# A recommendation kernel on one core: at most three gathers in flight, in place of eight

## The chip, the cores and the metric

The kernel runs on one NeuronCore of one Trainium2 chip. The core has a tensor engine (PE) for matrix products and transposes, a vector engine (DVE), a scalar engine (ACT) for activations, GpSimd (POOL), and a synchronisation engine (SP). SP, ACT and POOL can issue DMA transfers. In this kernel every gather of table rows is issued by POOL[...]; the 16 DMA engines of the core then move the rows. A semaphore tells when a transfer has landed.

The metric is device time in microseconds (us) of one launch, from the first to the last instruction. "The time before" is the median of three timed executions. Beside these stands one execution taken by the hardware profiler, with its own time.

## The reference

The model scores 16384 users (`B`), each with a target item and a history of 100 items (`L`), out of 50001 items (`ITEMS`). Every item has 32 neighbours. First each item gets two 32-wide vectors by attention over its neighbours, once for each of two tables; then each user is scored with a small attention network over the history.

```python
def _neighbor_attn(E, near_full):
    V = E[near_full]                                   # 50001 x 32 x 32
    scores = jnp.einsum('nd,nkd->nk', E, V) / jnp.sqrt(jnp.float32(GEO_HALF))
    w = jax.nn.softmax(scores, axis=-1)
    return jnp.einsum('nk,nkd->nd', w, V)
...
h = jnp.concatenate([E_hist[history], hist_bi], axis=-1)   # B x 100 x 128
t = jnp.concatenate([E_tgt[target], tgt_bi], axis=-1)      # B x 128
x = h * t[:, None, :]
z = jax.nn.relu(jnp.einsum('bld,hd->blh', x, W1) + b1)
scores = jnp.einsum('blh,h->bl', z, W2[0])
exp_A = jnp.exp(scores)
mask = (history != target[:, None]) & (history != 0)
exp_A = exp_A * mask
denom = jnp.sum(exp_A, axis=-1) ** BETA
...
s = jnp.sum(result)                # one number over all users
pred = dot / (n1 * n2)             # cosine of t with a vector of s
return jax.nn.sigmoid(pred)
```

All arithmetic is float32.

## The kernel before

The kernel has two stages and a short tail. Everything is laid out over 128 partitions.

**Stage 1, items.** 23 iterations (`NITER`) each cover 128 x 17 items (`NSUB` = 17). An iteration loads the neighbour indices (`nidx`), the items' own rows (`own`) and the history embeddings (`row`) by SP. For each of its 17 subtiles, 32 gathers (L111) bring one neighbour each for 128 items into a tile `v` of a five-buffer pool (64 floats a row). DVE multiplies (L120), reduces, ACT takes the exponentials, and DVE forms the weighted sum (L145, L152). At the end of an iteration SP writes the finished rows to two tables in DRAM, `table` (L163) and `ttab` (L164). There are 391 subtiles and so 12512 gathers. At the very start ACT also issues a 12.5 MB copy of the target embeddings into `ttab` (L91).

**Stage 2, users.** 128 users at a time, 128 such columns (`UC`). For each column one gather (L197) brings the target's rows `t`, and 100 gathers (L233) bring the history's rows, four to a group (`LG` = 4), 25 groups to a column (`NG`), into tiles `h` of a twelve-buffer pool (128 floats a row). That is 12800 gathers `h` and 128 gathers `t`, 25440 gathers in all with stage 1. A group then goes through:

- `turn`: four transposes on PE into `hT_ps` (L246), a DVE product with the transposed target into `xT` (L248), and a DVE row sum `hsum` (L249);
- `hidden`: a 128x128 by 128x512 product on PE into `z_ps` (L255), and a ReLU on ACT into `z` (L257);
- `scored`: four products on PE, one column each, into `score` (L265).

In the source these three stand one group apart (groups s, s-1 and s-2 in one turn of the loop). The program's layer that schedules the kernel takes this recording, decides in which order each engine gets its instructions by its own account of when their inputs are ready, and then sets semaphore waits. Engines run their lists strictly in that order. In the built program before, PE's usual order of a turn is: two transposes of a group, the first transpose of the next group, the first score product, a further transpose, three score products, and the product for `z`.

**Gathers in flight.** The layer gives the gathers eight semaphores in rotation. A gather waits until the gather eight places before it, the last user of its semaphore, has landed; the first eight of stage 1 wait for no gather. Where a tile's buffer is used again, the first gather into it also waits for the engines that read the old contents. Gathers run on POOL in the order of the program, and nothing else of weight runs on POOL.

Of the kernel before, what the change touches and what calls it, by code (L numbers as in the profile page):

```python
# [15 lines left out]

P = 128
ITEMS = 50001
K = 32
G = 32  # L20
DE = 64
# [8 lines left out]
NSUB = 17  # L30
NITER = -(-ITEMS // (P * NSUB))
ROWS = NITER * P * NSUB
# [10 lines left out]
def kernel(  # L43
# [11 lines left out]
    out: bass.AP,  # L55
):
    nc = tc.nc

    const = ctx.enter_context(tc.tile_pool(name="const", bufs=1))
    dram = ctx.enter_context(tc.tile_pool(name="dram", bufs=1, space=bass.MemoryType.DRAM))  # L60
# [29 lines left out]

    nc.scalar.dma_start(ttab[0 : ITEMS - 1, 0:DE], etgt[0 : ITEMS - 1, :])  # L91
    nc.scalar.dma_start(ttab[ITEMS - 1 : ITEMS, 0:DE], etgt[ITEMS - 1 : ITEMS, :])
    with (
        tc.tile_pool(name="n_in", bufs=2) as n_in,
        tc.tile_pool(name="n_v", bufs=5) as n_v,
        tc.tile_pool(name="n_p", bufs=2) as n_p,
        tc.tile_pool(name="n_s", bufs=3) as n_s,
        tc.tile_pool(name="n_ps", bufs=2, space=bass.MemoryType.PSUM) as n_ps,
    ):
        for it in range(NITER):  # L100
            nidx = n_in.tile([P, NSUB, K], I32, name="nidx")
            nc.sync.dma_start(nidx, near_v[it])
            own = n_in.tile([P, NSUB, 2 * G], F32, name="own")
            nc.sync.dma_start(own, egeo_v[it])
            row = n_in.tile([P, NSUB, D], F32, name="row")
            nc.sync.dma_start(row[:, :, 0:DE], ehist_v[it])
            trow = n_in.tile([P, NSUB, 2 * G], F32, name="trow")
            for j in range(NSUB):
                v = n_v.tile([P, K, 2, G], F32, name="v")
                for k in range(K):  # L110
                    nc.gpsimd.indirect_dma_start(  # L111
                        out=v[:, k].rearrange("p t d -> p (t d)"),
                        out_offset=None,
                        in_=egeo,
                        in_offset=bass.IndirectOffsetOnAxis(ap=nidx[:, j, k : k + 1], axis=0),
                    )
                own_ps = n_ps.tile([P, 1, 2 * G], F32, name="own_ps")
                nc.scalar.copy(own_ps[:, 0, :], own[:, j, :])  # L118
                prod = n_p.tile([P, K, 2, G], F32, name="prod")
                nc.vector.tensor_tensor(  # L120
                    prod.rearrange("p k t d -> p k (t d)"),
                    v.rearrange("p k t d -> p k (t d)"),
                    own_ps.to_broadcast([P, K, 2 * G]),
                    ALU.mult,
                )
                sc = n_s.tile([P, 2, K], F32, name="sc")
                nc.vector.tensor_reduce(sc.rearrange("p t k -> p k t"), prod, AX.X, ALU.add)  # L127
                top = n_s.tile([P, 2], F32, name="top")
                nc.vector.tensor_reduce(top, sc, AX.X, ALU.max)
                nc.vector.tensor_scalar(top, top, -scale, None, ALU.mult)  # L130
                ex = n_ps.tile([P, 2, K], F32, name="ex")
                tot = n_s.tile([P, 2, 1], F32, name="tot")
                for t in range(2):
                    nc.scalar.activation(  # L134
                        ex[:, t, :],
                        sc[:, t, :],
                        AF.Exp,
                        bias=top[:, t : t + 1],
                        scale=scale,
                        accum_out=tot[:, t, :],  # L140
                    )
                nc.vector.reciprocal(tot, tot)  # L142
                wv = n_p.tile([P, 2, G, K], F32, name="wv")
                for t in range(2):
                    nc.vector.tensor_tensor(  # L145
                        wv[:, t].rearrange("p d k -> p k d"),
                        v[:, :, t, :],
                        ex[:, t, :].rearrange("p (k o) -> p k o", o=1).to_broadcast([P, K, G]),
                        ALU.mult,
                    )  # L150
                att = n_s.tile([P, 2, G], F32, name="att")
                nc.vector.tensor_reduce(att, wv, AX.X, ALU.add)  # L152
                nc.vector.tensor_tensor(  # L153
                    row[:, j, DE:D].rearrange("p (t d) -> p t d", t=2),
                    att,
                    tot.to_broadcast([P, 2, G]),
                    ALU.mult,
                )
                for t in range(2):
                    nc.scalar.copy(  # L160
                        trow[:, j, t * G : (t + 1) * G], row[:, j, D - (t + 1) * G : D - t * G]
                    )
            nc.sync.dma_start(table_v[it], row)  # L163
            nc.sync.dma_start(ttab_v[it][:, :, DE:D], trow)  # L164
# [11 lines left out]
    with (  # L176
# [12 lines left out]
        def target_rows(c):  # L189

            if c % BSUB == 0:
                hidx = u_in.tile([P, BSUB, L], I32, name="hidx")
                nc.sync.dma_start(hidx, hist_v[c // BSUB])
                hists[c // BSUB] = hidx

            t = u_t.tile([P, D], F32, name="t")
            nc.gpsimd.indirect_dma_start(  # L197
                out=t,
                out_offset=None,
                in_=ttab[0:ITEMS, :],  # L200
                in_offset=bass.IndirectOffsetOnAxis(ap=tidx[:, c : c + 1], axis=0),
            )
            users[c] = {"t": t, "hidx": hists[c // BSUB][:, c % BSUB, :]}
# [24 lines left out]
        def gather(c, g):  # L228
            u = users[c]
            h = u_h.tile([P, LG, D], F32, name="h")  # L230
            for q in range(LG):
                l = g * LG + q
                nc.gpsimd.indirect_dma_start(  # L233
                    out=h[:, q, :],
                    out_offset=None,
                    in_=table,
                    in_offset=bass.IndirectOffsetOnAxis(ap=u["hidx"][:, l : l + 1], axis=0),
                )
            u["h", g] = h
# [37 lines left out]

        groups = [(c, g) for c in range(UC) for g in range(NG)]
        target_rows(0)
        for s in range(len(groups) + 2):  # L280
            if s < len(groups):
                c, g = groups[s]
                if g == 0:
                    target_work(c)
                if g == NG // 2 and c + 1 < UC:
                    target_rows(c + 1)
                gather(c, g)
                turn(c, g)
            if 1 <= s <= len(groups):
                hidden(*groups[s - 1])  # L290
            if s >= 2:
                scored(*groups[s - 2])
# [88 lines left out]
```

## Time and profile before

| | us |
|---|---|
| median of three timed runs | 36274.81 |
| lowest and highest of them | 36267.18, 36292.37 |
| the profiled execution's own time | 31810.23 |
| its span, first to last instruction | 31808.5 |
| stage 1 in the profile, first to last gather issue | 9.7 to 15626.3 |
| history gathers of stage 2, first to last issue | 15651.5 to 31787.6 |
| POOL busy in the span | 24005.7 (75%) |
| PE busy in the span | 15238.9 (48%, all but nothing of it in stage 1) |
| DVE busy | 8951.2 (28%) |
| ACT busy | 2851.2 (9%) |

The profiled execution took 4464.6 us less than the median of the timed runs. The page tells how the time of that one execution was spent; it tells nothing of how the timed ones differ from it.

A line of the groups reads: line of the kernel, engine, operation, what is written and read, how many | busy time in all, mean duration of one in ns | idle time of the engine just before them, and what ended most of it. In the digits of the 40 slices a 9 means 90% or more busy; the granted clock of PE is 1.0 in the first half and 0.5 for nearly all of the second. In the timeline a row begins with the start and the duration in us; several instructions of a kind are merged (x3), and brackets tell how long the engine had been idle and what ended it.

### The profile page before, as it was taken

The numbers are of one execution on the slowest core, as the hardware profiler recorded it, in microseconds if no ns is written. First come the engines' busy times: TensorE is split into PE (matmuls) and PEld (weight loads), VectorE is DVE, ScalarE is ACT, GpSimd is POOL, SyncE is SP. The second block draws the span as 40 slices with busy tenths as digits, with TensorE's granted clock in tenths as the row PEclk, the third lists the DMA queues.
The fourth block names the chain that finished last, engine by engine and source line by source line (L and its number), as shares of the span: only waits on it lengthen the run. The fifth ranks groups of instructions, "written<-read, shape, count | busy, mean of one in ns | idle before, by whom it ended". The sixth has DMA issues, their size and how long they took to land.

```text
span 31808.5 us, 154035 instructions
## 1 busy us (share of the span) xinstructions
PE 15238.9 (48%) x44931; PEld 9632.2 (30%) x44931; DVE 8951.2 (28%) x10957; ACT 2851.2 (9%) x6458; POOL 24005.7 (75%) x25446
## 2 busy tenths in 40 slices
PE   0000000000000000000299999999999999999999
PEld 0000000000000000000155555555555555555555
DVE  2222222222222222222222222222222222222222
ACT  0000000000000000000011111111111111111111
POOL 7777777777777777777777777777777777777777
PEclk9999999999999999999955555555555555555555
DMA  2111111111111111111122222222222222222221
GB/s 50 30 30 30 30 31 33 30 30 30 30 34 30 30 30 30 31 33 28 37 54 53 54 53 54 53 54 54 53 54 53 54 53 54 54 53 54 53 54 52
DMA packets 981064, 1358.75 MB, mean 43 GB/s; under 512 B 559872, under 2 KB 564352, under 8 KB 977280
## 3 DMA queue, kind: packets, MB, share of 16 engines
q0 software_dynamic: 814080, 1258.87, 17.1%
q1 hardware_dynamic: 115952, 77.16, 0.9%
q10 hardware_dynamic: 50192, 12.87, 0.2%
q8 instruction: 363, 5.95, 0.1%
q14 instruction: 477, 3.91, 0.0%
HBM read 1308.76 MB, written 51.30 MB: 43 GB/s over the span
## 4 chain that ended last, share of the span: by engine, by line
POOL 49%; issue 19%; PE 15%; DMA 14%; DVE 2%; ACT 1%; POOLq 0%; ACTq 0%; SPq 0%; DVEq 0%
POOL v L111 35%; POOL h L233 13%; DMA h<-table,hidx 11%; PE z_ps L255 7%; PE score L265 5%; PE hT_ps L246 3%; DMA v<-in_egeo_dram,nidx 2%; DVE xT L248 2%; ACT z L257 1%; POOL t L197 0%; POOLq L233 0%; DVE tT L211 0%; DVE ea L274 0%; DMA nidx<-in_near_dram 0%; DMA ttab<-trow 0%
## 5 line engine op out<-in xcount | busy, mean ns | idle before, releaser
L233 POOL DMA_INDIRECT h<-table,hidx x12800 | 12079.2, 944 | 3900.9 <-issue 3159.2
L111 POOL DMA_INDIRECT v<-in_egeo_dram,nidx x12512 | 11805.1, 943 | 3820.9 <-issue 3719.2
L209 PE MATMUL hT_ps<-ident,t 128*128 128x128 f32 x128 | 53.9, 421 | 15644.7 <-DMA t<-ttab,tidx 15644.7
L265 PEld LDWEIGHTS score<-w_sb,z 128*128 128x128 f32 x25600 | 6225.7, 334 | 1080.8 <-ACT z L257 1074.0
L255 PE MATMUL z_ps<-xT,w1T 128*128 128x512 f32 x6400 | 6526.7, 1123 | 0.0
L265 PE MATMUL score<-w_sb,z 128*128 128x1 f32 x25600 | 5903.9, 335 | 235.4 <-ACT z L257 150.2
L246 PE MATMUL hT_ps<-ident,h 128*128 128x128 f32 x12800 | 4715.0, 439 | 673.3 <-DMA h<-table,hidx 520.3
L249 DVE TENSOR_REDUCE hsum<-h 128x4 f32<-128x512 f32 x3200 | 2194.7, 686 | 9243.7 <-DMA h<-table,hidx 9226.9
L209 PEld LDWEIGHTS hT_ps<-ident,t 128*128 128x128 f32 x128 | 28.8, 225 | 15644.9 <-ACT idf L217 15644.9
L246 PEld LDWEIGHTS hT_ps<-ident,h 128*128 128x128 f32 x12800 | 2676.6, 209 | 5434.3 <-issue 3257.2
L120 DVE TENSOR_TENSOR prod<-v,own_ps 128x2048 f32<-128x2048 f32 x391 | 894.6, 2288 | 10794.7 <-DMA v<-in_egeo_dram,nidx 10794.4
L257 ACT ACTIVATE z<-z_ps,b_sb 128x512 f32<-128x512 f32 x3200 | 2199.1, 687 | 13448.3 <-PE z_ps L255 13335.1
L248 DVE TENSOR_TENSOR xT<-hT_ps,tT 128x512 f32<-128x512 f32 x3200 | 2210.2, 691 | 2028.6 <-PE hT_ps L246 2026.8
L255 PEld LDWEIGHTS z_ps<-xT,w1T 128*128 128x128 f32 x6400 | 1745.4, 332 | 0.0
L145 DVE TENSOR_TENSOR wv<-v,ex 128x1024 f32<-128x1024 f32 x782 | 1398.8, 1867 | 0.0
L118 ACT COPY own_ps<-own 128x64 f32<-128x64 f32 x391 | 84.4, 216 | 11499.9 <-DVE prod L120 11498.4
L127 DVE TENSOR_REDUCE sc<-prod 128x64 f32<-128x2048 f32 x391 | 894.5, 2288 | 13.4
L152 DVE TENSOR_REDUCE att<-wv 128x64 f32<-128x2048 f32 x391 | 893.8, 2286 | 13.4
L160 ACT COPY trow<-row 128x32 f32<-128x32 f32 x782 | 131.7, 215 | 2465.7 <-DVE row L153 2465.7
L134 ACT ACTIVATE ex<-sc,top 128x32 f32<-128x32 f32 x782 | 227.7, 291 | 1081.9 <-DVE top L130 1069.2
L142 DVE RECIPROCAL tot<-tot 128x2 f32<-128x2 f32 x391 | 64.8, 166 | 362.3 <-ACT ex L134 362.3
L197 POOL DMA_INDIRECT t<-ttab,tidx x128 | 120.7, 943 | 60.5 <-issue 60.5
(49 smaller groups left out, 808.6 us busy)
## 6 DMA issues: line engine op xcount, KB each, us to landing
h<-table,hidx POOLq DMA_INDIRECT x12800, 2.5
v<-in_egeo_dram,nidx POOLq DMA_INDIRECT x12512, 2.4
table<-row SPq DMA_DIRECT2D x23, 1088.0 KB, 4.4
own<-in_egeo_dram SPq DMA_DIRECT2D x23, 544.0 KB, 3.6
row<-in_ehist_dram SPq DMA_DIRECT2D x23, 544.0 KB, 6.7
ttab<-trow SPq DMA_DIRECT2D x23, 544.0 KB, 6.8
ttab<-in_etgt_dram ACTq DMA_DIRECT2D x1, 12500.0 KB, 53.5
hidx<-in_history_dram SPq DMA_DIRECT2D x32, 200.0 KB, 2.5
```

Source lines behind the costliest of these rows:

```text
L111: nc.gpsimd.indirect_dma_start(out=v[:, k].rearrange("p t d -> p (t d)"), out_offset=None, in_=egeo, in_offset=bass.IndirectOffsetOnAxis(a ...
L120: nc.vector.tensor_tensor(prod.rearrange("p k t d -> p k (t d)"), v.rearrange("p k t d -> p k (t d)"), own_ps.to_broadcast([P, K, 2 * G]), ...
L127: nc.vector.tensor_reduce(sc.rearrange("p t k -> p k t"), prod, AX.X, ALU.add)
L145: nc.vector.tensor_tensor(wv[:, t].rearrange("p d k -> p k d"), v[:, :, t, :], ex[:, t, :].rearrange("p (k o) -> p k o", o=1).to_broadcast ...
L152: nc.vector.tensor_reduce(att, wv, AX.X, ALU.add)
L233: nc.gpsimd.indirect_dma_start(out=h[:, q, :], out_offset=None, in_=table, in_offset=bass.IndirectOffsetOnAxis(ap=u["hidx"][:, l : l + 1], ...
L246: nc.tensor.transpose(hT_ps[:, q, :], h[:, q, :], ident)
L248: nc.vector.tensor_tensor(xT, hT_ps, u["tT"].to_broadcast([D, LG, P]), ALU.mult)
L249: nc.vector.tensor_reduce(u["hsum"][:, g * LG : (g + 1) * LG], h, AX.X, ALU.add)
L255: nc.tensor.matmul(z_ps, w1T, u["xT"].pop(g), start=True, stop=True)
L257: nc.scalar.activation(z, z_ps, AF.Relu, bias=b1_sb)
L265: nc.tensor.matmul(u["score"][:, l : l + 1], z[:, q, :], w2_sb, start=True, stop=True)
```

## The change

A wrapper, `gather_rows`, issues the gathers of all three places. It keeps a list of those issued, and from the fourth on it adds one dependency: the new gather waits until the gather three places before it has landed. The list runs over both stages. No instruction, no buffer and no transfer is added or taken away by the source; the layer that schedules the program sees the new dependencies when it decides the engines' orders, and drops waits that another one already covers.

```diff
+AHEAD = 3
...
+    issued = []
+    landed = mybir.DependencyInfo(mybir.DependencyClass.Sync, mybir.DependencyReason.DATA)
+
+    def gather_rows(**kw):
+        g = nc.gpsimd.indirect_dma_start(**kw)
+        if len(issued) >= AHEAD:
+            tc.add_manual_dep(g.ins, issued[-AHEAD].ins.name, landed, reason="AHEAD")
+        issued.append(g)
...
                 for k in range(K):
-                    nc.gpsimd.indirect_dma_start(
+                    gather_rows(
                         out=v[:, k].rearrange("p t d -> p (t d)"),
...
             t = u_t.tile([P, D], F32, name="t")
-            nc.gpsimd.indirect_dma_start(
+            gather_rows(
                 out=t,
...
                 l = g * LG + q
-                nc.gpsimd.indirect_dma_start(
+                gather_rows(
                     out=h[:, q, :],
```

In the built programs POOL has 25440 gathers before and after. Before, a gather's wait names the landing of the gather eight before it; after, that of the gather three before it, in the same place, so no wait is added in number (3745 waits that stand alone before, 3743 after). SP's order is unchanged. PE's order in stage 2 changes. After, most of it is a pattern that repeats every three groups (h a transpose, s a score product, digits the place in the group of four):

```
z(1)  h2.0 h2.1 h2.2  s1.0-s1.3  h2.3 h3.0 h3.1
z(2)  h3.2 h3.3       s2.0-s2.3  h4.0
z(3)  h4.1 h4.2 h4.3  s3.0-s3.3
z(4)  ...
```

Before, most turns are:

```
z(1)  h2.2 h2.3 h3.0  s1.0  h3.1  s1.1-s1.3
z(2)  h3.2 h3.3 h4.0  s2.0  h4.1  s2.1-s2.3
```

## The prediction

> **What bounds the kernel now.** I read the page's busy shares and chain first, then the groups, then one line's instructions, then the timeline.
>
> ```profile
> POOL 49%; issue 19%; PE 15%; DMA 14%; DVE 2%; ACT 1%; POOLq 0%; ACTq 0%; SPq 0%; DVEq 0%
> ...
> L233 POOL DMA_INDIRECT h<-table,hidx x12800 | 12079.2, 944 | 3900.9 <-issue 3159.2
> L111 POOL DMA_INDIRECT v<-in_egeo_dram,nidx x12512 | 11805.1, 943 | 3820.9 <-issue 3719.2
> ...
> h<-table,hidx POOLq DMA_INDIRECT x12800, 2.5
> v<-in_egeo_dram,nidx POOLq DMA_INDIRECT x12512, 2.4
> ```
>
> POOL leads the chain. A gather is busy 0.944 us and has an idle 0.30 us before it that ends by itself ("issue"), not by another's signal. The timeline shows the beat: starts at 6135-6145 below lie 1.25 us apart. Pace: (31787.6 - 9.7) us over 25440 gathers = 1.249 us, with a pause of only 23 us between the stages. The landing, 2.4 to 2.5 us from the start, comes after 2.45/1.249 = 2 beats. So about two gathers are in flight, although eight may be; it is POOL's issuing and not the limit that sets the pace.
>
> The exceptions are where large transfers share the DMA engines. For L111 between 6134 and 6146 us, and then from 9 to 52 us, its own rows say:
>
> ```profile
> DMA to landing us min/median/max: 2.5/4.3/5.5
> ...
> DMA to landing us min/median/max: 3.6/5.6/6.4
> ```
>
> ```profile
> 6134.74 0.33 SPq L163 DMA_DIRECT2D table<-row  x1
> 6134.93 0.94 POOL L111 DMA_INDIRECT v<-in_egeo_dram,nidx  x1 [0.30 <-issue]
> 6135.17 0.56 SPq L164 DMA_DIRECT2D ttab<-trow  x1
> 6136.18 0.94 POOL L111 DMA_INDIRECT v<-in_egeo_dram,nidx  x1 [0.30 <-issue]
> ...
> 6139.16 0.89 SPq L106 DMA_DIRECT2D row<-in_ehist_dram  x1
> ```
>
> Gathers land late beside the write-out of an iteration, and POOL keeps its beat nevertheless, since eight are allowed. In the first 52 us the 12.5 MB copy does the same.
>
> In stage 2 a second engine is close. The slices show PE at 9 with its clock at 5, and one turn of PE reads:
>
> ```profile
> 25001.99 2.06 PE L255 MATMUL z_ps<-xT,w1T 128*128 128x512 f32 x2
> 25003.83 0.85 PE L246 MATMUL hT_ps<-ident,h 128*128 128x128 f32 x3
> 25004.14 0.69 ACT L257 ACTIVATE z<-z_ps,b_sb 128x512 f32<-128x512 f32 x1 [4.63 <-PE z_ps L255]
> 25004.88 0.59 PE L265 MATMUL score<-w_sb,z 128*128 128x1 f32 x2 [0.20 <-ACT z L257]
> 25006.71 2.05 PE L255 MATMUL z_ps<-xT,w1T 128*128 128x512 f32 x2
> 25008.56 0.85 PE L246 MATMUL hT_ps<-ident,h 128*128 128x128 f32 x3
> 25008.87 0.69 ACT L257 ACTIVATE z<-z_ps,b_sb 128x512 f32<-128x512 f32 x1 [4.04 <-PE z_ps L255]
> 25009.23 0.69 DVE L248 TENSOR_TENSOR xT<-hT_ps,tT 128x512 f32<-128x512 f32 x1 [0.88 <-PE hT_ps L246]
> ```
>
> From three transposes to the next three is 4.73 us. The gathers allow a group 101 x 1.249/25 = 5.04 us (101 a column, 25 groups). PE has 0.31 us a group to spare.
>
> **What the Trainium skill says.** "DMA: Bandwidth & Descriptors", section "Anatomy of one DMA — SWDGE (gpsimd) path": about 2 us of a POOL-issued DMA is fixed, mostly completion, and engines of the DMA do not wait on semaphores; the issuer does. The trace agrees: 2.4 us of which 0.94 us is POOL's own. Same page, "Issuing engines are not separate DMA queues": SP's transfers interleave with POOL's on the same 16 engines; the 4.3 us beside the write-out agrees. "Perfetto Trace Analysis", section "DMA Instruction — SWDGE (GPSIMD)": the profiled end is that of descriptor writing, and an instruction sits in a wait queue until its semaphores are met, then in the execution queue. So the landing is to be taken from the issues' table, not from the 944 ns.
>
> **The change, part by part.**
>
> *The wait.* It replaces one; no instruction is added (25440 gathers, as many waits). Gather n may go when n-3 has landed. From the start of n-3: landing 2.45, plus about 0.28 us from signal to start (the first gather of all starts 0.28 us after the last semaphore event of its index transfer), together 2.73. Its turn comes after 3 x 1.249 = 3.75. It is met 1.0 us early, at no cost. What covers it is POOL's own work on the two gathers between; without it (two allowed, 2.50 of beats) each pair would lose 0.23 us. The wait queue of POOL holds only gathers behind this one.
>
> *Late landings.* Free up to 3.75 - 0.28 = 3.47 us. Beside each write-out some eight gathers land after about 4.5 us: three rounds of three, each 1.0 to 1.3 us late, 3 to 4 us an iteration; 23 iterations, 70 to 90 us. The first 44 us: a round takes 5.6 + 0.28 = 5.9 in place of 3.75, so 22 gathers go in place of 34: 15 us, some 20 with the loads just behind. At the profile's pace stage 1 loses about 100 us. POOL is the bound and nothing gives it back.
>
> *PE's order.* Signals from the rows above: `z` start to the scores that need it, 25004.88 - 25001.99 = 2.89 us. A transpose is 0.213 us of PE (three start at .213 spacing within the 0.85 row), four score products 1.71, `z` 1.85. From the start of a group's last transpose to its `xT` done and `z` starting: 0.46 + 0.69 + 0.06 = 1.21. Adding up the new three-group pattern: z, 3 transposes to 2.49, wait to 2.89 for ACT, scores to 4.61; last transpose then two others to 5.25, wait to 4.61 + 1.21 = 5.82 for DVE; z, two transposes to 8.10, wait to 5.82 + 2.89 = 8.71; scores to 10.43; one transpose; z at 10.64; three transposes, wait to 13.53; scores to 15.25. That is 5.08 us a group; before 4.73. So at the profile's pace PE passes POOL: (5.08 - 5.04) x 3200 = 130 us, and the target's transpose, once a column, is no longer hidden: up to 1 us x 128. Say 200 us, with late landings of stage 2 under it. Profile after: 31810 + 100 + 200 = 32,110.
>
> *At the pace of the timed runs.* They are 4465 us longer, 0.175 us a gather if spread over all. The page doesn't show where. If it is the beat of the gathers, it is 1.424 us: a group has 101 x 1.424/25 = 5.75 us, and PE's 5.08 is hidden by POOL again. Free landing grows to 4.27 - 0.28 = 3.99: beside a write-out rounds are 0.5 to 0.8 us late, 1.5 to 2.5 us an iteration, 35 to 58 us; at the start 22 gathers go in place of 31, 12 us; loads behind, 5 to 10. Sum 52 to 80, bounds 35 (signal to start at nothing) to 140 (nothing of it shrinks). I take 85, towards the slower side because the late gathers delay the tile that triggers the next write.
>
> **Rivals.**
> 1. *Forecast, 55%*: the beat is 1.42 us in timed runs. 36,275 + 85 = 36,360; its own range 36,310 to 36,415. For: two thirds of the chain is POOL and its issue; against: no view shows that beat.
> 2. *PE's new order shows, 22%*: stage 2 runs timed as profiled (the extra time lies in stage 1 or around). 100 + 200: 36,575, between 36,480 and 36,700.
> 3. *PE sets the timed runs' stage 2, 7%*: then 4.73 against 5.08 counts whole: 0.35 x 3200 = 1120, plus 100: 37,490. Against: PE would have to be over a third slower than at half clock.
> 4. *Landings are longer in timed runs, 8%*: from 3.99 us on, every 0.1 us costs 0.033 x 25440 = 850 us; at 4.1 us, 37,200.
> 5. *Faster, 6%*: the extra 0.175 us comes from gathers parked in POOL's queue, seven before and two after. It decides from 85/25440 = 0.0033 us a gather on; if a tenth goes, 0.0175 x 25440 = 445, less 85: 35,915. The profile's steady beat with the queue full speaks against it.
> 6. *Nothing happens, 2%*: landings beside the write-outs stay under the limit in timed runs: 36,275.
>
> **How the numbers follow.** 36,360 is case 1's. Cases 1, 2 and 6 hold 79%; a little of case 4 brings the range to 36,240 to 36,850. Within 0.2% (73 us, about what a measurement of this kernel can tell from no change): 42% of case 1, case 6 and a shred of 5, 0.26. Faster: 0.06. Slower: the rest, 0.68.
>
> **What would show it.** In the profile after, which has its own pace: L111's idle time is ended by "DMA v" for some 100 us at write-outs and in the first 52 us, and its plain beat stays 1.249; stage 2 longer by about 200 us, POOL waiting on buffers of `h`, PE waiting more for ACT `z` and for DVE `xT`. If POOL's beat is longer everywhere, the 0.28 us or the queue was misjudged. If stage 2 keeps 5.04 us a group, the PE sum is wrong. Timed runs beyond 36,480 make cases 2 to 4 likely; below 36,200, case 5.

## The result and the profile after

| | before | after |
|---|---|---|
| median of four timed runs each, us | 36275.44 | 36505.90 |
| lowest and highest, us | 36267.18, 36292.37 | 36500.71, 36511.53 |
| ratio, with its 95% interval | | 1.0063 (1.0046 to 1.0080) |

The change costs 230 us. The forecast was 36,360 in a range of 36,240 to 36,850. The time lies in the range, above the forecast's own range (36,310 to 36,415), and just inside the range of another case, that PE's new order shows (36,480 to 36,700).

The profile after was taken at the pace of these timed runs, whereas the profile before (31810.23 us) has the pace of the three chips of the experiments below, on which the unchanged kernel takes 31,808 us, timed as well as profiled; so the two profiles may not be subtracted from each other.

The page of the changed kernel, its busy times, its chain, the two groups of gathers and their issues:

```profile
PE 14440.2 (40%) x44931; PEld 9262.2 (25%) x44931; DVE 8694.6 (24%) x10957; ACT 2848.9 (8%) x6458; POOL 25501.7 (70%) x25446
...
PE 15%; another core or an unknown queue 12%; issue 4%; POOL 3%; DVE 2%; ACT 2%; DMA 1%; DVEq 0%; ACTq 0%; POOLq 0%
...
L65 POOL DMA_INDIRECT h<-table,hidx x12800 | 12078.1, 944 | 6655.3 <-issue 3380.1
L65 POOL DMA_INDIRECT v<-in_egeo_dram,nidx x12512 | 13302.2, 1063 | 4215.2 <-issue 4030.4
...
h<-table,hidx POOLq DMA_INDIRECT x12800
```

All gathers now have the wrapper's line, L65. The chain ends in releasers that the records do not name, and the landing that stood beside the issues before (2.5 us) is missing, because a part of the semaphore records is missing from this trace. What can be read is where the slower pace sits. In stage 1 (gathers of `v`) POOL's own duration has grown, 1063 ns in place of 943. In stage 2 (`h`) the duration is the old 944 ns, and the idle time before the gathers has grown from 3900.9 to 6655.3 us. All rows of L65 in the changed kernel:

```profile
L65 POOL DMA_INDIRECT v<-in_egeo_dram,nidx x12512: 938/949/1937, 8.4 to 17516.9; - x199
...
  issue: 7463.7, 22899
  remote: 2024.1, 790
  PE hT_ps L257: 641.5, 306
  DMA h<-table,hidx: 234.5, 655
```

The first row gives the lowest, median and highest duration in ns: over half of the gathers of stage 1 are as short as before. Counted from the trace, 44% take over 1.0 us, up to 1.94, and these repeat with the tile: of its 32 gathers the first takes 1.86 us on average, the fifteenth to the twenty-first 0.94. The last rows give what ended POOL's idle time, in us and times: 790 waits of some 2.6 us have no releaser in the records, and 306 wait for the transposes that free a buffer. The timeline shows one of these stalls:

```profile
25005.94 0.94 POOL L65 DMA_INDIRECT h<-table,hidx  x1 [0.30 <-issue]
25010.02 0.69 ACT L268 ACTIVATE z<-z_ps,b_sb 128x512 f32<-128x512 f32 x1 [12.96 <-remote]
25010.76 1.86 PE L276 MATMUL score<-w_sb,z 128*128 128x1 f32 x8 [9.23 <-ACT z L268]
...
25013.22 0.94 POOL L65 DMA_INDIRECT h<-table,hidx  x1 [6.33 <-PE hT_ps L257]
```

ACT stands for 12.96 us with no cause that the trace shows, PE waits for its `z`, and POOL then waits 6.33 us for PE to free a buffer of `h`. Between such stalls the beat of stage 2 is 1.249 us, as before. So the slower pace is not one longer beat for all gathers. At the end of the span, after the last gather, only the work of PE, DVE and ACT is left, and the ReLU shows its beat:

```profile
36446.56 0.69 ACT L268 ACTIVATE z<-z_ps,b_sb 128x512 f32<-128x512 f32 x1 [4.04 <-PE z_ps L266]
...
36461.79 0.69 ACT L268 ACTIVATE z<-z_ps,b_sb 128x512 f32<-128x512 f32 x1 [4.04 <-PE z_ps L266]
...
36477.01 0.69 ACT L268 ACTIVATE z<-z_ps,b_sb 128x512 f32<-128x512 f32 x1 [4.04 <-PE z_ps L266]
```

The rows lie three groups apart, 15.22 us, or 5.07 us a group. The last gather starts 69.9 us before the end (20.8 in the profile before), so PE is some ten groups further behind there.

### The profile page after: what moved, and what is told of

Same layout as the page of the kernel before. It is cut to its first block, busy times and chain, and to the rows that moved or that the text cites. A ratio compares the mean times of both kernels' runs of the same rounds, so it can differ in the third digit from the quotient of the medians.

```text
span 36505.5 us, 154118 instructions
## 1 busy us (share of the span) xinstructions
PE 14440.2 (40%) x44931; PEld 9262.2 (25%) x44931; DVE 8694.6 (24%) x10957; ACT 2848.9 (8%) x6458; POOL 25501.7 (70%) x25446
## 5 line engine op out<-in xcount | busy, mean ns | idle before, releaser
L65 POOL DMA_INDIRECT h<-table,hidx x12800 | 12078.1, 944 | 6655.3 <-issue 3380.1
L65 POOL DMA_INDIRECT v<-in_egeo_dram,nidx x12512 | 13302.2, 1063 | 4215.2 <-issue 4030.4
L266 PE MATMUL z_ps<-xT,w1T 128*128 128x512 f32 x6400 | 6197.3, 1070 | 2580.8 <-DVE xT L259 2473.7
L276 PE MATMUL score<-w_sb,z 128*128 128x1 f32 x25600 | 5700.5, 344 | 1921.9 <-ACT z L268 1422.8
L276 PEld LDWEIGHTS score<-w_sb,z 128*128 128x128 f32 x25600 | 5426.7, 313 | 3158.3 <-ACT z L268 2205.0
L257 PEld LDWEIGHTS hT_ps<-ident,h 128*128 128x128 f32 x12800 | 2966.2, 246 | 3488.6 <-issue 3436.4
L257 PE MATMUL hT_ps<-ident,h 128*128 128x128 f32 x12800 | 3810.0, 416 | 10.5 <-DMA h<-table,hidx 9.6
L266 PEld LDWEIGHTS z_ps<-xT,w1T 128*128 128x128 f32 x6400 | 1658.0, 318 | 3044.1 <-DVE xT L259 2874.1
L65 POOL DMA_INDIRECT t<-ttab,tidx x128 | 120.7, 943 | 63.6 <-issue 53.2
```

The costliest lines, as they stand in the source:

```text
L65: g = nc.gpsimd.indirect_dma_start(**kw)
L257: nc.tensor.transpose(hT_ps[:, q, :], h[:, q, :], ident)
L266: nc.tensor.matmul(z_ps, w1T, u["xT"].pop(g), start=True, stop=True)
L276: nc.tensor.matmul(u["score"][:, l : l + 1], z[:, q, :], w2_sb, start=True, stop=True)
```

## The experiments

The changed kernel has two things mixed: the limit, and the new order of PE in stage 2. The first four runs take them apart. In the tables a difference is the kernel's median less the median of the unchanged kernel on the same chip. The last columns come from the trace: the time from the first to the last start of a gather of each stage, less that of the unchanged kernel (15616.9 and 16138.3), and the tail, from the last gather to the end of the span. The changed kernel is left out of these columns: its profiled execution took 32181.04 us, 59 more than its median, with its gathers at 946 ns in place of 944. Two in flight was profiled with the same 946 ns, which is small beside its difference.

| kernel | median us | difference | ratio (95%) | stage 1 | stage 2 | tail us |
|---|---|---|---|---|---|---|
| unchanged (its profiled execution) | 31809.53 | | | | | 20.8 |
| limit in stage 1 alone | 31946.24 | +137.6 | 1.0044 (1.0030 to 1.0057) | +135.5 | -0.9 | 20.7 |
| limit in stage 2 alone | 31985.21 | +176.6 | 1.0056 (1.0042 to 1.0069) | -0.2 | +171.8 | 19.6 |
| PE's new order, no limit | 31894.27 | +85.7 | 1.0027 (1.0016 to 1.0037) | -0.3 | +35.6 | 67.3 |
| limit, PE's old order | 32111.99 | +304.4 | 1.0095 (1.0078 to 1.0112) | +137.3 | +171.9 | 20.7 |
| the changed kernel | 32121.96 | +314.3 | 1.0099 (1.0082 to 1.0115) | | | |
| four in flight | 31868.51 | +59.7 | 1.0019 (1.0011 to 1.0026) | +30.0 | +29.3 | 20.1 |
| five in flight | 31811.76 | +2.9 | 1.0001 (0.9993 to 1.0009) | +3.8 | +0.7 | 20.7 |
| PE's old order held, no limit | 31808.61 | -0.3 | 1.0000 (0.9991 to 1.0008) | -0.5 | -0.6 | 20.8 |
| two in flight | 36813.67 | +5006 | 1.1574 (1.1551 to 1.1597) | +1435.5 | +3581.0 | 19.3 |

### The pace of the unchanged kernel

No edit.

> The kernel before, unchanged, profiled once more: at which pace does it run where timed runs take 36275 us? If the beat of the gathers is slower throughout (the forecast's case), gathers start every 1.42 us in both stages and stage 1 takes some 17,800 us. If the extra time sits in stage 1 alone, stage 1 takes some 20,100 us and stage 2 16,140. If PE sets stage 2, stage 2 takes some 20,600 us and PE is busy nearly all of it. If this execution comes out at 31,810 us again, the profiler itself speeds the kernel up and nothing is told of the timed runs.

> The kernel before, unchanged, profiled on the chip of this call. If that chip takes 36,275 us: gathers 1.42 us apart throughout (the forecast's case) or stalls in one stage alone. If it takes 31,809 us: the same profile as before, with gathers 1.249 us apart.

> The kernel before, unchanged, for its profile beside these runs: 31,808 us if this chip has the pace of the profile before, 36,275 us if it has that of the first timed runs.

Measured: 31809.53, 31807.77 and 31808.92 us, on three chips, and the medians of the timed runs on them (31808.61, 31807.62, 31808.86) are the same within 1 us. The profiled execution of the changed kernel, 36507.29 us, agrees with its timed runs too. So nothing points to the profiler as what made the profile before 4465 us shorter than its timed runs. What makes the pace of the first timed runs is not known: none of these runs met it.

### The limit in one stage at a time

Against the changed kernel:

```diff
 # stage 1 alone
-            gather_rows(            # t
+            nc.gpsimd.indirect_dma_start(
...
-                gather_rows(        # h
+                nc.gpsimd.indirect_dma_start(
```

```diff
 # stage 2 alone
-                    gather_rows(    # v
+                    nc.gpsimd.indirect_dma_start(
```

> The limit of three in stage 1 alone; every engine's order is that of the kernel before. Late landings (the forecast): the whole of the +230 us measured comes from here, or at least +85 (35 to 140): 36,310 to 36,505. PE's new order (rival 2): up to +100 here and the rest in stage 2. The limit in stage 2 itself: 0 here, 36,275.

> The limit of three in stage 2 alone; the engines' orders are those of the changed kernel. Late landings (the forecast): 0 to +10, 36,275 to 36,285. PE's new order (rival 2): +130 to +230, 36,405 to 36,505. The limit in stage 2 itself, whatever PE's order: the same +130 to +230, so that the next run has to tell the two apart.

Measured: +137.6 and +176.6 us, together 314.2, and the changed kernel as a whole loses 314.3. The parts add up and both stages pay. PE has its old order in the first of the two kernels and its new one in the second, so the second does not yet tell the limit from the order. The groups of the kernel with the limit in stage 1 alone:

```profile
L244 POOL DMA_INDIRECT h<-table,hidx x12800 | 12078.0, 944 | 3900.9 <-issue 3067.7
L65 POOL DMA_INDIRECT v<-in_egeo_dram,nidx x12512 | 11804.4, 943 | 3956.7 <-issue 3720.6
```

and that of `h` with the limit in stage 2 alone:

```profile
L65 POOL DMA_INDIRECT h<-table,hidx x12800 | 12077.6, 944 | 4072.0 <-issue 3152.7
```

The durations stand still; only idle time grows, in the first kernel 3956.7 in place of 3820.9 for `v`, with `h` at the old 3900.9, and in the second 4072.0 for `h`. Where this idle time lies in stage 1 can be read at a write-out (it comes later by then, at 6202 us), and, in the second view, over the first 60 us:

```profile
6202.99 0.94 POOL L65 DMA_INDIRECT v<-in_egeo_dram,nidx  x1 [1.34 <-DMA v<-in_egeo_dram,nidx]
6205.35 0.94 POOL L65 DMA_INDIRECT v<-in_egeo_dram,nidx  x1 [1.42 <-DMA v<-in_egeo_dram,nidx]
6206.60 0.94 POOL L65 DMA_INDIRECT v<-in_egeo_dram,nidx  x1 [0.30 <-issue]
6208.52 0.94 POOL L65 DMA_INDIRECT v<-in_egeo_dram,nidx  x1 [0.98 <-DMA v<-in_egeo_dram,nidx]
```

```profile
  DMA v<-in_egeo_dram,nidx: 22.0, 17
...
DMA to landing us min/median/max: 2.6/5.7/6.5
```

Three gathers of this write-out wait for a landing, 1.04, 1.12 and 0.68 us longer than the usual 0.30. I took the starts of all gathers of stage 1 from the trace and summed what each period has over 1.248: 16 us in the first 58 us, 63 us within 16 us after a write-out (2.7 each, 23 of them), 10 us beside the loads of an iteration. That is 89 us. The other 47 us lie on single gathers, at gather numbers 113, 219, 325 and so on, counted from 0: one in 106, always 7 more than a multiple of 106, whether or not a large transfer is near.

### PE's order without the limit, and the limit without PE's order

In both kernels `turn`, `hidden` and `scored` are cut into single instructions, which are issued in an order written down beforehand and held. The first takes the changed kernel's order and leaves the limit out; the second takes the order of the kernel before and has the limit.

```diff
+        for op in ORDER:      # "h", "s", "z", "T", one letter per instruction of PE
+            n = at[op]
+            at[op] += 1
...
-                nc.tensor.transpose(hT_ps[:, q, :], h[:, q, :], ident)
+            tc.keep_in_program_order(nc.tensor.transpose(hT_ps[:, q, :], h[:, q, :], ident))
```

> No limit at all (eight in flight as before), but PE's instructions pinned in exactly the order that the changed kernel has. PE's new order (rival 2): +130 to +230, 36,405 to 36,505, as in the run with the limit in stage 2. Late landings, or the limit in stage 2 itself: 0, 36,275.

> The limit of three in both stages, but PE's instructions pinned in exactly the order that the kernel before has. On a chip where the kernel before takes 31,809 us: if what stage 2 loses is PE's new order (rival 2), only the late landings are left, +138 as the limit in stage 1 alone cost, and up to 30 for stage 2: +140 to +170, 31,950 to 31,980. If the limit itself costs in stage 2 whatever PE's order, all of it stays: +310, 32,120. On a chip where the kernel before takes 36,275 us: late landings alone +60 to +140; if the limit itself is what counts there, the whole +230.

> The changed kernel as it is, on the chip of this call. On a chip at 31,809 us the two halves should add up, since they follow each other in time: 138 + 177 = +315, 32,125 (the prediction's own sum for that pace was +300, 32,110). On a chip at 36,275 us: +230 as measured, 36,506.

> No limit, PE's order written down as it was in the kernel before and held. It tells what holding an order costs by itself, in the runs that held one. If nothing, 0 us (within 10) against the kernel before; if it costs what the runs with a held order lost, up to +86 us.

Holding an order costs nothing by itself (31808.61 against 31808.86). The new order alone costs 86 us, between what the two expectations allowed for (0, or 130 to 230). The limit with PE's old order costs 304 us, of which 172 lie in stage 2; the changed kernel, with the new order, costs 314. So stage 2 loses its 172 us to the limit itself, and PE's order adds about 10. (With the limit in stage 2 alone PE has the new order too, and its tail is 19.6 us: PE keeps up.) The page of the kernel with the new order and no limit, its gathers of stage 2, and the longest of their waits that PE ends:

```profile
L238 POOL DMA_INDIRECT h<-table,hidx x12800: 938/944/1037, 15651.4 to 31822.7; - x197
...
  PE hT_ps L255: 204.7, 572
```

The last gather starts at 31822.7 and the span ends at 31890.0: a tail of 67.3 us, where it was 20.8. PE falls behind POOL until twelve buffers are full of groups that it hasn't worked off; only then does POOL wait (35.6 us in all; the 204.7 of the view hold the usual 0.30 us of each of its 572 gathers), and what PE still owes is the longer tail (46.5 us). From the first gather of stage 2 to the end PE has taken (16173.9 + 67.3)/3200 = 5.075 us a group, the target's transposes included.

And the kernel with the limit and PE's old order, first its groups, then POOL near 22877 us; after it the unchanged kernel at the same gathers:

```profile
L70 POOL DMA_INDIRECT h<-table,hidx x12800 | 12079.5, 944 | 4070.1 <-issue 3315.5
L70 POOL DMA_INDIRECT v<-in_egeo_dram,nidx x12512 | 11804.1, 943 | 3959.2 <-issue 3721.1
```

```profile
22873.68 0.94 POOL L70 DMA_INDIRECT h<-table,hidx  x1 [0.30 <-issue]
22874.92 0.94 POOL L70 DMA_INDIRECT h<-table,hidx  x1 [0.30 <-issue]
22876.17 0.94 POOL L70 DMA_INDIRECT h<-table,hidx  x1 [0.31 <-issue]
22879.58 0.94 POOL L70 DMA_INDIRECT h<-table,hidx  x1 [2.47 <-DVE hsum L273]
22880.83 0.94 POOL L70 DMA_INDIRECT h<-table,hidx  x1 [0.30 <-issue]
...
23144.82 0.94 POOL L70 DMA_INDIRECT h<-table,hidx  x1 [0.30 <-issue]
23146.53 0.94 POOL L70 DMA_INDIRECT h<-table,hidx  x1 [0.77 <-issue]
```

```profile
22663.44 0.94 POOL L233 DMA_INDIRECT h<-table,hidx  x1 [0.30 <-DMA h<-table,hidx]
22664.69 0.94 POOL L233 DMA_INDIRECT h<-table,hidx  x1 [0.30 <-issue]
22665.94 0.94 POOL L233 DMA_INDIRECT h<-table,hidx  x1 [0.30 <-issue]
22667.19 0.94 POOL L233 DMA_INDIRECT h<-table,hidx  x1 [0.30 <-issue]
```

The gather at 22879.58 is number 18133 (7 + 171 x 106), and that at 23146.53 is number 18345, two such places further. The first comes 3.41 us after the gather ahead of it, the second 1.71 us, where 1.25 is the beat; the releaser that the view names for the first, `hsum`, had been done: this gather writes a buffer that is used again and has a wait instruction of its own, and POOL's rows show that instruction at 22876.3 us with 43 ns, 3.3 us before the gather starts. In the unchanged kernel the same gather starts on its beat, at 22665.94.

To see what they wait for, I compared each gather's start with the landing of the gather three before it. An ordinary gather that is held up starts 0.26 us after that landing. A gather whose buffer is used again has a wait instruction of its own ahead of it; it starts 0.76 us after. A gather of the one-in-106 kind mostly starts 1.73 us after it in stage 1, with a few at 2.5. In stage 2 it goes by the place in the group of four: the third and fourth start some 1.73 us after, the second mostly some 2.5, and the first, which has a wait of its own too, 3.34. The mean of these gathers' periods, and what they have in all over the beat:

| kernel | stage 1, 118 of them | stage 2, 122 of them |
|---|---|---|
| unchanged | 1.248, 0 us | 1.248, 0 us |
| limit in stage 1 alone | 1.648, 47 us | 1.249, 0 us |
| limit in stage 2 alone | 1.248, 0 us | 2.338, 132 us |
| limit, PE's old order | 1.664, 49 us | 2.344, 133 us |
| the changed kernel, over its beat of 1.251 | 1.670, 49 us | 2.331, 132 us |
| four in flight | 1.264, 2 us | 1.489, 29 us |
| five in flight | 1.257, 1 us | 1.248, 0 us |

So of the 172 us that stage 2 loses, 133 lie on one gather in 106. The other 39 lie scattered, on some 190 ordinary gathers that are held up a little.

### Two, four and five in flight

```diff
-AHEAD = 3
+AHEAD = 2      # and 4, and 5
```

> At most two gathers in flight, in both stages. The price of the wait by the forecast's formula: two gathers take the landing and the signal, 2.43 + 0.26 = 2.69 us in stage 1 and 2.77 in stage 2, in place of 2.50. That is 0.10 us a gather in stage 1 and 0.13 in stage 2, some 1200 + 1700 us, and the late landings on top (each round of two loses about 3 us at a write-out: 200 to 300 in all): 34,900 to 35,100 on a chip at 31,809 us. If the formula is wrong and the two beats cover the landing, under 32,500. On a chip at 36,275 us: if landings there are as long as here and only the beat is slower, hardly more than three in flight, under 36,900; if landings are longer there as well, over 38,000.

> The same with four in flight; cover 4 x 1.249 = 5.0 us. Theory, pauses no longer covered: the plain pause (4.17 us) is hidden; where it falls on a gather with a wait of its own (5.78) 0.8 us show, some 25 times, 20 us; in the first 52 us rounds of four take 5.86 in place of 5.0, about 7 us; beside a write-out only landings over 4.74 are late, 20 to 30 us over 23 of them. Sum +45 us. PE has a new order here too, which may add up to the 86 us that the other new order cost by itself: bounds +30 to +130. Rival, a cost at each gather: about +300 us.

> The limit in both stages as in the changed kernel, but five gathers in flight in place of three. PE's order is the old one but for 13 places. Theory, pauses no longer covered: five allowed give 5 x 1.249 = 6.24 us of cover. The pause that comes once in 106 gathers (2.43 + 1.73 = 4.17 us from start to the start that waits) is hidden, the pause that falls on a gather with a wait of its own (2.43 + 3.34 = 5.78) is hidden, late landings (5.6 + 0.26 = 5.86) are hidden but for the longest of 6.4 in the first 52 us. So within +0 to +15 us of the kernel before. Rival, a wait on a nearer gather costs something at each gather: about as much as with three, +300 us.

Measured: +5006, +59.7 and +2.9 us. Four and five came out as the theory of pauses that are no longer covered has it: five cover 6.24 us of beats and hide everything, four (5.0 us) hide the plain pause (2.45 + 1.73 = 4.2) but not the one that falls on a gather with a wait of its own (2.45 + 3.3 = 5.8), and the trace of four has 29 us on the gathers of that kind in stage 2, 25 of them on firsts of a group, and hardly any in stage 1, where some 27 us of late landings are left. A cost at each gather, the rival, would have stayed near +300. PE has a new order with four too, another than the changed kernel's, and it costs nothing that shows: its tail is 20.1 us. The groups with five in flight have the idle time of the unchanged kernel (3900.9 and 3820.9) but for 4 us:

```profile
L65 POOL DMA_INDIRECT h<-table,hidx x12800 | 12079.1, 944 | 3901.3 <-issue 3440.6
L65 POOL DMA_INDIRECT v<-in_egeo_dram,nidx x12512 | 11804.6, 943 | 3824.2 <-issue 3718.6
```

Two in flight missed its expectation by some 1,800 us. Its groups, and POOL's two longest sums of waits:

```profile
L65 POOL DMA_INDIRECT h<-table,hidx x12800 | 12109.7, 946 | 7358.3 <-DMA h<-table,hidx 5309.5
L65 POOL DMA_INDIRECT v<-in_egeo_dram,nidx x12512 | 11834.5, 946 | 5226.5 <-DMA v<-in_egeo_dram,nidx 4724.8
```

```profile
POOL h L65 <- DMA h<-table,hidx: 5309.5, 8495, 3.0
POOL v L65 <- DMA v<-in_egeo_dram,nidx: 4724.8, 11504, 4.3
```

Here landings rule both stages. In stage 1 an ordinary pair takes 2.64 us in the median, the landing and the start there (2.37 + 0.26 = 2.63), or 1.32 a gather. The mean over the stage is 1.363; that is no beat, as 180 of the 1435.5 us lie on one gather in 106 and 203 on the first gathers of tiles, which have a wait of their own, and more on late landings. Stage 2 has a mean of 1.525: of its 3581 us, some 2300 lie on 3093 first gathers of groups, which have a wait of their own and start 0.76 us after the landing (2.46 + 0.76 - 2.50 = 0.72 each by the sum, 0.74 measured), 250 on one in 106, 111 on gathers of `t` and some 940 on ordinary ones. PE has yet another order there, but a group takes 6.16 us, well over the 5.075 that PE needed in the changed kernel's order. The expectation had priced neither a wait of its own nor the one in 106.

## Why the prediction was right, and where it was not

**POOL's beat bounds both stages, and the wait itself is free.** Shown at the pace of the profile before. With the limit the durations stay 943 and 944 ns, and some 98% of the gathers keep the beat of 1.249 us (limit, PE's old order). The start 0.28 us after a signal, read from one gather, is 0.26 over many. But it holds for ordinary gathers alone, and not for the one in 106.

**Late landings, "about 100 us" in stage 1 at the profile's pace.** The size was right, the terms nearly so: 15 to 20 us at the start measured 16; 70 to 90 at the write-outs measured 63; loads measured 10. Together 89. The stage loses 137, and what the sum did not have is the 47 us of the one gather in 106.

**PE's order, "say 200 us" in stage 2 at the profile's pace, "with late landings of stage 2 under it".** This step failed. Its number was near (stage 2 loses 172 to 177), its cause was not. The pattern's 5.08 us a group was well worked out: the order alone ran at 5.075. But that already holds the target's transposes, for which the 200 us added up to 1 us each, and 86 is what the order cost. And the cover was the wrong way round: with the limit the gathers need (16138.3 + 171.9)/3200 = 5.097 us a group, more than PE's 5.075, so it is PE's order that lies under the limit's stalls. With PE's old order restored, 304 of 314 us stay.

**The wait of one gather in 106.** It was not in the working at all. Nothing in the profile before could show it: with eight in flight these gathers start on their beat. It makes 49 + 133 = 182 of the 304 us.

**The sum at the profile's pace, 32,110.** Measured 32,122 on a chip of that pace. It came out by luck: a term that was too large (PE) stood in the place of one that was missing.

**The beat of 1.42 us in timed runs.** This step failed in its form. The trace at that pace has a beat of 1.249 us in 88% of the periods of stage 2 and in about half of those of stage 1; the time lies in longer single gathers in stage 1 and in stalls of ACT and PE in stage 2. So the free landing did not grow to 3.99 us for the gathers between, and "+85" was too small; that the time lies in the whole range is owed to the width that other cases gave it. In the profile after, the gathers of the one-in-106 kind take 1.69 us on average in stage 1 and 2.33 in stage 2, against 1.40 and 1.45 for all others: (0.29 x 118) + (0.88 x 122) = 141 us. It is of the size of what the forecast lacks (230 - 85 = 145), but as there is no profile of the kernel before at that pace, this split is argued, not shown, and PE's order is a rival to it.

**The rivals.** The case "PE's new order shows" has the range nearest to the time, and on the chips of the experiments its mechanism makes about 10 of the 314 us. At the pace of the timed runs this is open: the tail of the profile after is 69.9 us, like that of the run with PE's new order alone, so PE is behind there and works off its groups at 5.07 us each between stalls, and the order's share was not measured at that pace. Longer landings would have cost 850 us for each 0.1 us beyond 3.99, and 925 us at 4.1: the measured 230 leaves no room for them as the rule, though the profile after has no landings recorded to read them from. A gain from an emptier queue did not come either: on the chips of the experiments five in flight run as eight do.

**The price of two in flight, 0.23 us a pair.** Right for a plain pair of stage 2, whose median is 2.72 us (0.22 over 2.50). In stage 1, where the landing takes 2.37 us and not 2.45, a plain pair loses 0.14; that the mean of that stage comes to 0.23 a pair is luck, made of the terms named above. In stage 2 as a whole 0.55 a pair is lost (0.277 a gather), since every second pair there begins with a wait of its own and takes 3.2 us.

## What to carry to other kernels

A limit on transfers in flight has to cover the slowest landing and start, not the usual ones: here 2.45 us of landing and 0.26 us to start asked for three at a beat of 1.249 us, but one start in 106 takes 1.7 us, or 3.3, landings beside a large transfer came late as well, and of three, four and five only five made the limit free. A profile in which a queue is deep cannot show such starts, as they are met in advance; so before a queue is made shallower, try two or three depths, and look at single long periods rather than at means. When an order and a wait change together, hold the order and change the wait alone: the numbers of two causes can be alike, as they were in stage 2.

## What the runs showed of the hardware that was not expected

- One indirect gather on POOL in 106, counted from the first of the program and across both stages, starts 1.73 us or more after the landing it waits for, in place of 0.26 us. With the signal early enough it costs nothing. What POOL does there is not shown.
- A wait that stands as an instruction of its own ahead of a gather raises the start after the landing from 0.26 to 0.76 us, and together with the one in 106 to about 3.3 us.
- The same kernel takes 31,808 us on three chips, with a profile or without one, and 36,275 us in the first timed runs. At the slower pace single gathers of stage 1 take up to 1.94 us, at fixed places of a tile, and in stage 2 ACT stands still 213 times before a `z`, for 7 us on average and once for 35, with no releaser in the records. The cause is open.
